# Layer 1's projection of two tiles by seven block products in place of eight

## Chip, core and metric

The kernel runs on one core of one Trainium2 chip. The metric is the device time of one execution in microseconds (us). The engines are named as in the profile: PE (matrix products; PEld is its weight load), DVE (vector), ACT (scalar and tables), POOL (which here issues the gathers) and SP (which issues the other transfers).

## The reference

Two graph attention layers follow one another on 3327 nodes with 1024 features. Each layer's output is added to its input, and the sum is normalized over the features.

```
# layer 0: 8 heads of 128
h = x @ W0;  e[h,i,j] = leaky(h_i . a_src[h] + h_j . a_dst[h]);  masked by adj
x = layernorm(x + softmax(e) @ h)
# layer 1: one head
h = x @ W1;  e[i,j] = leaky(h_i . a1 + h_j . a2);  masked by adj
x = layernorm(x + relu(softmax(e) @ h))
```

The adjacency matrix is sparse (about 0.5% set, plus the diagonal). All data are fp32.

## The kernel before, in words

The 3327 rows are cut into 26 tiles of 128 (`NT`). The program has three stages. The first projects x with W0 (L475), turns the adjacency into lists of edges and stores the projected rows in `h0_d`. A flag then picks one of two forms; with this input it is `sparse` (L743), which does layers 0 and 1 with gathers.

In `sparse` each target tile has four blocks of 4 x 128 edges (`NG` = 4 groups of 32 targets) and a last block of 128 edges. `gather` (L800) fetches the source row of every edge by indirect DMAs, 17 per tile, on POOL's queue. Blocks share five buffers `src0` to `src4`. `weights` makes the attention weights of one block on DVE, and `sums` multiplies them with the gathered rows on PE.

Layer 1 (`Target`, L940) first aggregates the normalized rows y, and then projects: (attention @ y) @ W1 is the same as attention @ (y @ W1). `sums` (L987) adds up three cuts of 342, 342 and 341 columns in three banks. `close` (L998) divides by the sum of the weights and adds the node's own row; the result is z. `finish` (L1015) transposes z in two halves on PE (L176, copied to `xT` by ACT, L179), multiplies xT by W1, which stands in SBUF as `wt1` (eight blocks of 128 rows), in two halves of 512 columns (L1025), and applies maximum and residual on DVE (L1028). `settle` (L1033) normalizes and stores.

`prepare` (L946) loads a tile's own rows y, makes the marks that say which edge belongs to which target (L819, L823), and brings the target's scores into the layout of `way`, by a transposition (L949) and an exponential (L951). `way` is one bank of PSUM which holds small intermediate values for both layers.

The order of all work is written out by hand in `pipeline` (L1038), under a manual schedule: every engine executes its instructions in the order in which they are emitted, and waits for the data of the others. For tile t and block b, it emits in this order: at block 0 the `close` of tile t-1, then `late` steps of the queue `work`; `prepare` of tile t+1 at block 2; `own` at block 0; `weights` of block b+1; `sums` of block b; the gathers of block b of tile t+1; `behind[b]` steps of `work`; and one step of `ahead`. `work` holds the generators `finish`, `ahead` the generators `settle` (and, at first, `score_weights`, L767). A step runs to the next `yield`. In layer 1 a tile's `finish` has ten steps, two for the transpositions and eight for a quarter of a half projection each; `late` is 1 and `behind` is (2, 2, 2, 2, 1).

PSUM has eight banks. Before, tag A has five of them (accumulators of both layers), S one (projection, and layer 0's denominator), T one (transpositions), and E one (`way`). In layer 0 the two accumulators of a tile come from A, in layer 1 the three.

Of the kernel before, what the change touches and what calls it, by code (L numbers as in the profile page):

```python
# [19 lines left out]
P = 128  # L20
# [6 lines left out]
def kernel(  # L27
# [43 lines left out]
    EB = 4  # L71
# [671 lines left out]
    def sparse(own):  # L743
        ph = Phase(own, "sparse", {"A": 5, "S": 1, "T": 1, "E": 1})
# [20 lines left out]
        wa = [pool.tile([P, D], F32, bufs=1, name=f"wa{n}") for n in range(2)]  # L765

        def score_weights():  # L767
            for n, a in enumerate((a1_src, a1_dst)):
                av = sbuf("z", [P, D], 3, "av")
                spread(av, a)  # L770
                for k in range(KT):
                    pr = sbuf("pr", [P, D], 1)
                    nc.vector.scalar_tensor_tensor(
                        pr, wt1[:, k, :], 1.0, av, op0=OP.mult, op1=OP.mult, accum_out=wc[:, n, k : k + 1]
                    )
                    if k % 3 == 2:
                        yield
# [48 lines left out]
        class Layer0:  # L826
# [5 lines left out]
            def prepare(self):  # L832
# [4 lines left out]
                self.h = sbuf("own", [P, HW0], 2)  # L837
# [14 lines left out]
            def begin(self):  # L852
                self.acc = [bank("A", [P, 4, DH], "acc") for _ in range(2)]
# [4 lines left out]
            def weights(self, b):  # L858
# [10 lines left out]
                e = sbuf("e", [P, H * P], 3).rearrange("p (g h t) -> p g h t", g=ng, h=H)  # L869
# [45 lines left out]
            def finish(self):  # L915
# [13 lines left out]
                for n in range(2):  # L929
                    pr = sbuf("pr", [P, D], 1)  # L930
                    nc.vector.scalar_tensor_tensor(  # L931
                        pr, y, 1.0, wa[n], op0=OP.mult, op1=OP.mult, accum_out=r1.sd[:, t, n, :]
# [7 lines left out]
        class Target:  # L940
# [5 lines left out]
            def prepare(self):  # L946
                t = self.t
                tr = bank("T", [P, P], "tr")
# [6 lines left out]
                self.res = ys[t % 3]  # L955
# [15 lines left out]
            def begin(self):  # L971
                self.acc = [bank("A", [P, CUTS[1]], "acc1") for _ in range(3)]
# [25 lines left out]
            def close(self):  # L998
# [5 lines left out]
                z = self.z = sbuf("z", [P, D], 3)  # L1004
# [10 lines left out]
            def finish(self):  # L1015

                t, z, res = self.t, self.z, self.res
                xT = sbuf("xT", [P, KT, P], 2)
                yield from ph.transposed(xT, z, (0, 1))
                o = sbuf("z", [P, D], 3, "o")  # L1020
                for g in range(2):
                    half = slice(g * HALF, (g + 1) * HALF)
                    acc = bank("S", [P, HALF], "mm")
                    for k in range(KT):
                        nc.tensor.matmul(acc, xT[:, k, :], wt1[:, k, half], start=k == 0, stop=k == KT - 1)  # L1025
                        if k in (1, 3, 5):
                            yield
                    nc.vector.scalar_tensor_tensor(o[:, half], acc, 0.0, res[:, half], op0=OP.max, op1=OP.add)  # L1028
# [203 lines left out]
```

## Time and profile before

| | us |
|---|---|
| median of 3 runs | 1957.28 (1956.42 to 1968.05) |
| profiled execution | 1903.19 |
| its span, first to last instruction | 1901.5 |
| PE busy | 1518.5 (80%) |
| DVE busy | 1146.6 (60%) |
| POOL busy | 1030.2 (54%) |
| ACT busy | 546.6 (29%) |
| PE, projection of layer 1 (L1025) | 383.3, 832 records |
| PE, sums of layer 1 (L993) | 206.2, 2496 records |

The profile is of one execution, taken by the hardware profiler. Times in it count from the span's start. Layer 0's gathers begin at 482 us, those of layer 1 at 1198.6; layer 1 ends with the span. An fp32 product of one weight block appears as two matmul records. Busy time of PE is modelled, since its products are pipelined; the chain of waits shows their real spacing. The chain follows the work that ended last back to what released it.

### The profile page before, as it was taken

The numbers are of one execution on the slowest core, as the hardware profiler recorded it, in microseconds if no ns is written. First come the engines' busy times: TensorE is split into PE (matmuls) and PEld (weight loads), VectorE is DVE, ScalarE is ACT, GpSimd is POOL, SyncE is SP. The second block draws the span as 40 slices with busy tenths as digits, with TensorE's granted clock in tenths as the row PEclk, the third lists the DMA queues.
The fourth block names the chain that finished last, engine by engine and source line by source line (L and its number), as shares of the span: only waits on it lengthen the run. The fifth ranks groups of instructions, "written<-read, shape, count | busy, mean of one in ns | idle before, by whom it ended". The sixth has DMA issues, their size and how long they took to land.

```text
span 1901.5 us, 38079 instructions
## 1 busy us (share of the span) xinstructions
PE 1518.5 (80%) x14663; PEld 902.4 (47%) x14663; DVE 1146.6 (60%) x3058; ACT 546.6 (29%) x1422; POOL 1030.2 (54%) x1391
## 2 busy tenths in 40 slices
PE   8799999999266555656556565399999999999997
PEld 5465556666255554545545454144444444444443
DVE  6699999986386665666666666244444444444442
ACT  5544455542022222222222222012222212222220
POOL 4322222220576666676676764677766667666650
PEclk9899999999678777787788877699999999999999
DMA  7656455411899999999999997899999999999980
GB/s 184 101 133 131 100 99 99 88 62 39 325 373 404 396 392 394 366 405 392 386 392 389 394 376 273 332 398 410 400 372 382 380 378 369 359 371 373 366 326 33
DMA packets 171068, 567.76 MB, mean 299 GB/s; under 512 B 27690, under 2 KB 34346, under 8 KB 170878
## 3 DMA queue, kind: packets, MB, share of 16 engines
q0 software_dynamic: 131056, 455.68, 67.6%
q1 hardware_dynamic: 39822, 109.56, 15.4%
q8 instruction: 118, 1.93, 0.4%
q14 instruction: 72, 0.59, 0.1%
HBM read 578.85 MB, written 42.97 MB: 327 GB/s over the span
## 4 chain that ended last, share of the span: by engine, by line
PE 52%; DMA 24%; DVE 12%; ACT 6%; issue 4%; POOL 2%; SPq 0%; DVEq 0%; ACTq 0%; POOLq 0%
DMA src<-h_d,idx 20%; PE mm L1025 20%; PE acc L993 12%; PE mm L479 12%; DVE e L870 3%; PE acc L898 3%; ACT junk L311 3%; PE tr L176 2%; POOL src L803 2%; DMA src<-y_d,idx 2%; DVE pr L931 1%; PE acc L882 1%; DMA wt<-in_L_gnn_W_dram 1%; ACT xT L179 1%; PE xp L411 1%
## 5 line engine op out<-in xcount | busy, mean ns | idle before, releaser
L803 POOL DMA_INDIRECT src<-h_d,idx x416 | 441.1, 1060 | 209.1 <-PE acc L898 58.0
L803 POOL DMA_INDIRECT src<-y_d,idx x416 | 415.7, 999 | 221.6 <-PE acc L993 96.3
L898 PE MATMUL acc<-src,e 128*32 128x128 f32 x6656 | 278.5, 337 | 253.6 <-DVE e L870 253.5
L479 PE MATMUL mm<-wt,xT 128*128 128x347 f32 (+1 forms) x1248 | 402.3, 469 | 3.3 <-DMA wt<-in_L_gnn_W_dram 2.9
L1025 PE MATMUL mm<-wt,xT 128*128 128x512 f32 x832 | 383.3, 604 | 0.8 <-DVE o L1028 0.8
L898 PEld LDWEIGHTS acc<-src,e 128*32 128x32 f32 x6656 | 234.8, 137 | 311.3 <-DVE e L870 284.3
L479 PEld LDWEIGHTS mm<-wt,xT 128*128 128x128 f32 x1248 | 228.3, 192 | 106.0 <-issue 4.2
L1025 PEld LDWEIGHTS mm<-wt,xT 128*128 128x128 f32 x832 | 152.2, 190 | 199.5 <-issue 179.1
L993 PE MATMUL acc<-src,es 128*32 128x342 f32 (+1 forms) x2496 | 206.2, 464 | 33.8 <-DVE es L984 31.0
L870 DVE TENSOR_TENSOR e<-oh,way 128x1024 f32<-128x1024 f32 x130 | 158.7, 1221 | 63.2 <-ACT w L868 62.8
L993 PEld LDWEIGHTS acc<-src,es 128*32 128x32 f32 x2496 | 71.6, 111 | 158.6 <-issue 112.9
L868 ACT ACTIVATE w<-way 128x32 f32<-128x32 f32 (+1 forms) x130 | 24.6, 189 | 407.7 <-DVE way L866 395.6
L1028 DVE SCALAR_TENSOR_TENSOR o<-mm,y 128x512 f32<-128x512 f32 x52 | 35.9, 691 | 166.2 <-PE mm L1025 166.2
L1007 ACT ACTIVATE z<-y,ri 128x342 f32<-128x342 f32 (+1 forms) x78 | 39.5, 570 | 313.9 <-DVE ri L1003 313.9
L865 DVE TENSOR_TENSOR way<-src,re 128x32 f32<-128x32 f32 x104 | 20.8, 200 | 175.1 <-DMA src<-h_d,idx 157.6
L179 ACT ACTIVATE xT<-tr 128x512 f32<-128x512 f32 x104 | 59.4, 596 | 151.0 <-PE tr L176 150.9
L981 DVE TENSOR_TENSOR way<-way,src 128x128 f32<-128x128 f32 x104 | 31.1, 299 | 90.0 <-ACT way L951 44.2
L850 ACT ACTIVATE own<-own,es 128x128 f32<-128x128 f32 x208 | 63.6, 388 | 57.4 <-DVE es L847 57.4
L311 ACT ACTIVATE junk<-ad 128x3328 uint8<-128x3328 uint8 x26 | 78.4, 3014 | 2.5 <-POOL ad L308 2.5
L882 PE MATMUL acc<-end,e 128*128 128x128 f32 x416 | 67.7, 328 | 13.3 <-DVE e L870 13.3
L296 POOL CAST mvs<-r 128x8 bf16<-128x8 f32 x26 | 6.0, 232 | 122.8 <-ACT r L295 122.8
L335 POOL TENSOR_TENSOR place_of<-cnt 128x1 f32<-128x1 f32 x26 | 4.9, 190 | 121.0 <-ACT cnt L328 101.5
(188 smaller groups left out, 1959.7 us busy)
## 6 DMA issues: line engine op xcount, KB each, us to landing
h_d<-ht SPq DMA_DIRECT2D x26, 520.0 KB
own<-h_d SPq DMA_DIRECT2D x26, 520.0 KB
y_d<-y SPq DMA_DIRECT2D x26, 514.0 KB
y<-y_d SPq DMA_DIRECT2D x26, 514.0 KB
x<-in_x_dram SPq DMA_DIRECT2D x25, 512.0 KB
y<-in_x_dram SPq DMA_DIRECT2D x25, 512.0 KB
out_dram<-o SPq DMA_DIRECT2D x25, 512.0 KB
ad<-in_adj_dram POOLq DMA_DIRECT2D x25, 415.9 KB
```

The costliest lines, as they stand in the source:

```text
L176: nc.tensor.transpose(tr[:, k, :], src[:, (4 * g + k) * P : (4 * g + k + 1) * P], ident)
L179: nc.scalar.activation(part, tr, AF.Copy)
L311: nc.scalar.activation(junk, ad, AF.Copy, accum_out=self.deg)
L479: nc.tensor.matmul(acc, xT[t][:, k, :], wt[:, k, CUTS0[c] : CUTS0[c + 1]], start=k == 0, stop=k == KT - 1)
L803: nc.gpsimd.indirect_dma_start(out=s[:, g, :w], out_offset=None, in_=table[:, :], in_offset=bass.IndirectOffsetOnAxis(ap=idx[:, t, b * NG ...
L850: nc.scalar.activation(hn, hn, AF.Copy, scale=es[:, n : n + 1])
L870: nc.vector.tensor_tensor(e, oh.unsqueeze(2).to_broadcast([P, ng, H, wide]), wp.unsqueeze(3).to_broadcast([P, ng, H, wide]), OP.mult,)
L882: nc.tensor.matmul(self.acc[h // 4][:, h % 4, :], e[:, 0, h, :], rowsof[:, 0, h, :], start=False, stop=h % 4 == 3,)
L898: nc.tensor.matmul(self.acc[h // 4][g * GT : (g + 1) * GT, h % 4, :], e[:, g, h, :], rowsof[:, g, h, :], start=first and h % 4 == 0, stop= ...
L993: nc.tensor.matmul(self.acc[c][to, :m], es[:, g, :], s[:, g, CUTS[c] : CUTS[c + 1]], start=b == 0, stop=b == EB,)
L1007: nc.scalar.activation(z[:, cut], self.res[:, cut], AF.Copy, scale=ri[:, 1:2])
L1025: nc.tensor.matmul(acc, xT[:, k, :], wt1[:, k, half], start=k == 0, stop=k == KT - 1)
```

## The change

Two consecutive tiles of layer 1, an even one a and an odd one b, are projected together. With xT and W1 each cut into blocks of half the inner dimension and half the columns, four blocks of the result take eight products of blocks in the plain way. The new code makes seven, after Strassen in Winograd's form. Each has four inner blocks of 128, so 16 steps of `finish` with two inner blocks each become 14.

- `combine_weights` forms four combinations of the blocks of W1, once, between the two layers. They are kept in `on_marks` with `prod` (t2, t3), in `owns` (t4), and in `wt1` itself (w12). These are buffers which layer 0 has used.
- `first` makes two products for the even tile: the first one is copied to u2 by ACT, the second gives a's first half.
- `second` makes four combinations of xT on DVE, five products, and from these b's two halves and a's second half. A half is finished by `put`: one addition, and the maximum with the residual, in place in the tile's rows `res`.
- `settle` normalizes in place in `res`. The rows y of layer 1 have five buffers in place of three (the two vectors `wa` of layer 0 get reused), z has one in place of three, and the vector `av` of `score_weights` has one as well.
- The banks: A 3, S 3, T 1, E 1. Layer 1's accumulators use the three of A, its products those of S. In layer 0 the accumulators take A and A, or A and S, in turn. The transposition of the scores in layer 1's `prepare` writes to a free quarter of `way`.
- `pipeline` takes other numbers of steps for even and odd tiles, the first being `late`: (2, 1, 1, 2, 2, 2) and (2, 2, 1, 2, 1, 0). `lag=4` puts four empty steps first; no steps are taken behind tile 0. Layer 0 keeps its steps.

```diff
-        ph = Phase(own, "sparse", {"A": 5, "S": 1, "T": 1, "E": 1})
+        ph = Phase(own, "sparse", {"A": 3, "S": 3, "T": 1, "E": 1})
...
-        wa = [pool.tile([P, D], F32, bufs=1, name=f"wa{n}") for n in range(2)]
+        was = [pool.tile([P, HW], F32, bufs=1, name=f"wa{n}") for n in range(2)]
+        wa = [w[:, :D] for w in was]
+        owns = [pool.tile([P, HW0], F32, bufs=1, name=f"own{n}") for n in range(2)]
+        on_marks = [pool.tile([P, D], F32, bufs=1, name=f"e{n}") for n in range(3)]
+        prod = pool.tile([P, D], F32, bufs=1, name="prod")
+        HK = KT // 2
+        w11, w12 = wt1[:, :HK, :HALF], wt1[:, :HK, HALF:]
+        w21, w22 = wt1[:, HK:, :HALF], wt1[:, HK:, HALF:]
...
+        def combine_weights():
+            for n in range(2):
+                k = slice(2 * n, 2 * n + 2)
+                nc.vector.tensor_tensor(t3[n], w22[:, k, :], w12[:, k, :], OP.subtract)
+            nc.vector.tensor_tensor(w12, w12, w11, OP.subtract)
+            for n in range(2):
+                k = slice(2 * n, 2 * n + 2)
+                nc.vector.tensor_tensor(t2[n], w22[:, k, :], w12[:, k, :], OP.subtract)
+                nc.vector.tensor_tensor(t4[n], w21[:, k, :], t2[n], OP.subtract)
...
-                av = sbuf("z", [P, D], 3, "av")
+                av = sbuf("z", [P, D], 1, "av")
...
-                self.acc = [bank("A", [P, 4, DH], "acc") for _ in range(2)]
+                self.acc = [bank(tag, [P, 4, DH], "acc") for tag in ("AA", "AS")[self.t % 2]]
...
-                tr = bank("T", [P, P], "tr")
+                tr = way[:, 3 * P :]
...
-                self.res = ys[t % 3]
+                self.res = y1s[t % len(y1s)]
...
-                self.acc = [bank("A", [P, CUTS[1]], "acc1") for _ in range(3)]
+                self.acc = {c: bank("A", [P, CUTS[1]], "acc1") for c in (2, 0, 1)}
...
+                self.xT = sbuf("xT", [P, KT, P], 2)
+                turn = ph.transposed(self.xT, self.z, (0, 1))
+                next(turn)
+                yield
+                next(turn)
+                yield from self.second() if self.t % 2 else self.first()
+
+            def product(self, a, w):
+                self.p = bank("S", [P, HALF], "mm")
+                for k in range(HK):
+                    nc.tensor.matmul(self.p, a[:, k, :], w(k), start=k == 0, stop=k == HK - 1)
+                    if k == 1:
+                        yield
+
+            def put(self, g, u, p, room):
+                half = slice(g * HALF, (g + 1) * HALF)
+                nc.vector.tensor_tensor(room, u, p, OP.add)
+                nc.vector.scalar_tensor_tensor(
+                    self.res[:, half], room, 0.0, self.res[:, half], op0=OP.max, op1=OP.add
+                )
+
+            def first(self):
+                yield
+                yield from self.product(self.xT, lambda k: w11[:, k, :])
+                nc.scalar.activation(u2, self.p, AF.Copy)
+                yield
+                yield from self.product(self.xT[:, HK:, :], lambda k: w21[:, k, :])
+                self.put(0, u2, self.p, u4)
+                yield
+
+            def second(self):
+                before = tiles1[self.t - 1]
+                a, b = before.xT, self.xT
+                a1, a2, b1, b2 = a[:, :HK, :], a[:, HK:, :], b[:, :HK, :], b[:, HK:, :]
+                nc.vector.tensor_tensor(s1, b1, b2, OP.add)
+                nc.vector.tensor_tensor(s2, s1, a1, OP.subtract)
+                nc.vector.tensor_tensor(b1, a1, b1, OP.subtract)
+                nc.vector.tensor_tensor(a2, a2, s2, OP.subtract)
+                yield
+                yield from self.product(s2, lambda k: t2[k // 2][:, k % 2, :])
+                nc.vector.tensor_tensor(u2, u2, self.p, OP.add)
+                yield
+                yield from self.product(s1, lambda k: w12[:, k, :])
+                p5 = self.p
+                nc.vector.tensor_tensor(u4, u2, p5, OP.add)
+                yield
+                yield from self.product(b1, lambda k: t3[k // 2][:, k % 2, :])
+                nc.vector.tensor_tensor(u3, u2, self.p, OP.add)
+                self.put(1, u3, p5, u2)
+                yield
+                yield from self.product(b2, lambda k: t4[k // 2][:, k % 2, :])
+                self.put(0, u3, self.p, u3)
+                ahead.append(self.settle())
+                yield
+                yield from self.product(a2, lambda k: w22[:, k, :])
+                before.put(1, u4, self.p, u4)
+                ahead.append(before.settle())
+                yield
...
-                    run(work, behind[b])
+                    if t:
+                        run(work, behind[b])
...
-            pipeline(Layer0, 0, (1, 1, 1, 1, 1), get_edges)
-            pipeline(Target, 1, (2, 2, 2, 2, 1), lambda t: None)
+            pipeline([Layer0(t) for t in range(NT)], ((0, 1, 1, 1, 1, 1),) * 2, get_edges)
+            combine_weights()
+            tiles1 = [Target(t) for t in range(NT)]
+            y1s = ys + was
+            pipeline(tiles1, ((2, 1, 1, 2, 2, 2), (2, 2, 1, 2, 1, 0)), lambda t: None, lag=4)
```

## The prediction

> **What bounds the kernel now.** I read the windows by stage first, then the chain of waits inside layer 1, then the waits and the DMA rate. The windows (columns: window and its length, busy PE, PEld, DVE, ACT, POOL, granted clock, DMA share, GB/s):
>
> ```profile
> 480.00:840.00 360.00, 208.47 (x3985) 173.84 (x3989) 223.27 (x538) 81.62 (x242) 242.53 (x230) 0.77 1.00 384
> ...
> 1400.00:1540.00 140.00, 136.56 (x767) 58.80 (x766) 61.31 (x178) 30.80 (x54) 94.15 (x95) 1.00 0.99 378
> ...
> 1409.86:1435.41 25.55, 24.86 (x145) 10.68 (x144) 11.37 (x33) 5.84 (x12) 17.00 (x18) 1.00 0.99 371
> ```
>
> Layer 0 (480 to about 1193) has PE busy 58% and DMA full; the change's products are not there. Layer 1 has PE busy 97% at full clock, and DMA nearly full as well. The last row is exactly one layer-1 tile: 25.55 us, DVE busy 11.4. The chain through that tile (start, length, what):
>
> ```profile
> 1409.86 3.43 PE mm L1025 x8
> 1413.30 1.86 PE acc L993 x24
> 1415.16 0.60 PE tr L176 x4
> 1415.76 0.02 issue
> 1415.79 0.61 ACT xT L179
> 1416.39 0.04 issue
> 1416.44 0.66 PE tr L176 x4
> 1417.09 1.86 PE acc L993 x24
> 1418.95 3.63 PE mm L1025 x8
> ...
> 1433.68 1.73 PE acc L993 x6
> ```
>
> The reader is to see that one tile is PE work end to end, with one hole of 0.68 us (second transposition waiting for ACT). It gives the units: half a product P (four records) is 1.71 us; a pair of P is 3.43, or 3.63 directly after a sums block; sums S 1.86, last block E 1.73, transposition of half a tile T 0.66. From the waits and the rate at the start of layer 1, where POOL issues without pause:
>
> ```profile
> POOL src L803 <- PE acc L993: 91.4, 104, 3.7
> ACT xT L179 <- PE tr L176: 117.3, 42, 4.8
> PE tr L176 <- ACT xT L179: 14.5, 21, 0.7
> ...
> 1215.00:1220.00 5.00, 3.78 (x5) 0.63 1.03 416
> 1220.00:1225.00 5.00, 3.78 (x5) 1.00 1.03 410
> 1240.00:1245.00 5.00, 3.94 (x4) 1.00 1.02 408
> ```
>
> Gathers wait for PE to free their buffers, and no wait on a gather is left in steady layer 1. But the ceiling is near: about 410 GB/s. A tile moves 376 GB/s (mean of four tiles) x 25.55 us = 9.61 MB, so DMA alone needs 23.4 us per tile. POOL needs 17 gathers x 1.295 us between starts = 22.0.
>
> **What the Trainium skill says.** "Perfetto Trace Analysis", Identifying the Most-Contended Engine: PE's matmul busy share is a bad measure of headroom, since matmuls are pipelined. Hence I take spacing from the chain (0.43 us per record), not the 592 ns that one record shows; the trace agrees that these differ. "VectorE: DVE Perf Modes", Mode 2x_2P: an fp32 tensor_tensor stays at one element per cycle. The trace agrees: L870 takes 1.22 us for 1024, L819 0.68 for 512. "PSUM — Partial Sum Buffer", PSUM bank collisions raise a hardware error: two engines may not touch one bank at once, so accesses must be guarded by bank. The trace shows such a guard: DVE L981 waits for ACT L951, which writes other columns of `way` (40.6 us in 21 times).
>
> **The change, part by part.**
>
> *Products.* Per pair of tiles 14 P instead of 16. Before, a pair takes 51.1 us. After, in PE's order by the counts. Odd tile: P P (3.43), S, P P (3.63), S, T, S, T, P (1.75), S, P (1.91), E. Even tile: P P (3.43), S, T, S, T, S, P P (3.63), S, P P (3.63), E, P P (3.43). P sums to 24.8, eight S and two E to 18.3, four T to 2.65, the two score transpositions to 0.2: 46.0 us. The saving of 5.1 has two roots: 3.9 in products, 1.2 because the two T of a tile now have sums between them.
>
> *Additions on DVE.* Eleven tensor_tensor of 128x512 per pair more (four combinations of xT, three of u, four in put); the four maxima stay. Price 0.69 each (L1028 0.69, L819 0.68); 0.61 start to start if the next one does not depend on it, 0.72 if it does. Some 7.6 us per pair, so DVE goes from 11.4 to about 15.2 us per tile: not full, but in order. I walk it against PE:
> (a) Into the odd tile. After the third product of `second` DVE does u3 and put (0.1+0.72+0.72+0.61), and only then close (three small ones 0.6, ACT's first z, then three STT every 0.51). The first STT ends 3.9 us, the last 4.95 after that product; PE arrives at the sums after 3.43. Accumulators now have three banks, so all three wait: 0.57 us.
> (b) Odd tile, block 0 to 2. After the last product DVE does put (1.4), the statistics of one settle (1.7), then weights(2) (0.96) : 4.2 us. PE meanwhile has S and T, 2.5. The stall is 1.7; the score transposition, now in the bank of `way`, has to wait as well and adds 0.2 (bounds 0 and 0.3). 1.9 us.
> (c) Into the even tile: put, own, weights(1) 2.8 against S and T 2.5: 0.35.
> Other places hold, some barely: s2 is ready about when PE gets to it. Some 0.2 for that. Stalls 3.0 (bounds 1.5 and 4.5, if DVE's gaps are 20% smaller or such a place turns bad). Pair: 49.0, or 24.5 per tile, above DMA's 23.4. Gain 2.0 (51.1 - 46.0 - 3.0 = 2.1, rounded down for the tighter DMA); twelve pairs, 24.
>
> *ACT.* One copy u2 (0.6) per pair, beside PE's work; its covers are the P after it. If uncovered 0.6.
>
> *Start of layer 1.* combine_weights: 8192 elements per partition, six of 1.22 and one of about 2.4, 9.7 us on DVE. It is queued after the last normalization (1193.3), ahead of the marks. DVE waits 14.74 us there for the first gather (to 1208.9), marks take 1.0. It hides with 4 us to spare: 0 (bounds 0 and 9.7). Four empty steps keep tile 1 light; it then runs at the gathers' speed: 1.2 less.
>
> *End.* After the last sums PE had 3.43 + two T + 16 records x 2; now P P, two T, a wait for ACT, s1, s2 (2.2), and five products (17.1), then two settles one after the other (3.2 each) instead of one. I get 38.5 against 32.0 (1869.5 to 1901.5): +6.5.
>
> *Layer 0.* Own rows, marks and product buffers are the same rings under other names; accumulators return after two tiles instead of 2.5, den after two instead of one. No wait there names a free bank; 0. But av has one buffer: the load of the second vector waits for the last product of the first (530.2) and SP's later loads queue behind it; DVE then waits for it in front of tile 1's weights. Loads there take 4 to 12 us (y_d 4.1, own 11.9), before DVE needed it at 532.7. Later DVE is full until 560 and gathers pause. Bounds 0 and 6; I take 2.
>
> *Queues.* SP issues one load and one store per tile as before, two stores per pair close together. The load of y at block 2 has about 14.5 us until the next tile's own (18.5 before); nobody waited for it in 540 us, own<-h_d took 11.9 in layer 0. Nothing taken; a late one would stop DVE in front of weights(1).
>
> **Sum.** -24 - 1.2 + 6.5 + 2 = -16.7. Profiled: 1903.2 (span 1901.5 and 1.7 around it) to 1886.5. The median shown is 54 us above that execution, and no view says where these lie. Difference or ratio give 1940.6 and 1940.1: 1940.
>
> **Rivals.** A is the forecast: stalls 1.5 to 4.5 give 1921 to 1957.
> B, the stalls vanish, and the gathers become the bound: 23.4 per tile, pair 46.8, 12 x 4.3 = 51 less 7.3 of one-off costs: 1914. For it: DVE has 9 us per tile free even afterwards, so its backlog is short. Against: (a) and (b) come from the order of DVE's queue, which is fixed by the code, not from its load.
> C, slower: DVE's additions lie bare on PE's path at tile boundaries, since each accumulator has only one bank. All 7.6 bare: pair 53.7, +31 + 7.3 = +38: 1996. It decides from 4.5 us of stalls per pair (5.1 less 7.3/12). Against: places other than (a) to (c) have 3.4 us of products as cover.
> D, no gain: the 54 us of the timed runs are slow transfers. On layer 0's 700 us that is 7.7%, the ceiling becomes 381 GB/s, a tile 25.2 us: 24 x 0.35 = 8 less 7.3: 1957. For it: DMA at 0.99 already. Against: in the trace 410 holds in both layers.
> That seven products aren't made is ruled out: two in `first`, five in `second`, four blocks of 512 columns each.
>
> **Chances.** A 0.5, B 0.2, C 0.12, D 0.18. One per cent (19.6 us) is about what a measurement can tell from no change. Faster by more: B and two fifths of A, 0.40; same: the rest of A and D, 0.48; slower: C. Range 1914 to 1966: from B to a little over D; outside are C and a part of B.
>
> **What would show it.** Pair period near 49 instead of 51.1; waits of PE for DVE L982/L984 of about 1.9 at one block per pair and for DVE's z of 0.6; DVE about 63% in layer 1; gathers still waiting for PE; 38 us after the last sums; DVE's first weights of layer 1 not after 1209. Wrong if PE waits for gathers (B or D), or if stalls pass 4.5 per pair.

## The result, and the profile after

The changed kernel took 2026.64 us (median of six runs, 2018.09 to 2031.58); beside it the kernel before took 1960.4 (1952.59 to 1970.13). The ratio is 1.0338, interval 1.0315 to 1.0362: slower, against a forecast of 1940. The numbers below come from seven comparisons, each of which ran the kernel before beside a changed one: in two of them the kernel before took 1960 and 1984 us, in the other five 1900 to 1902, with no lower granted clock (in the second slower one 0.91 to 0.92, in the faster ones 0.90 to 0.92), and I call them the slower and the faster comparisons. The result above is a slower one. The profile of before (1903) is of the faster kind, its median (1957) of the slower.

The windows of the changed kernel's first profile (2028.36 us, span 2026.6, from the slower comparison), in the stages shown of before (window and length; busy PE, PEld, DVE, ACT, POOL, each with its number of instructions; granted clock, DMA share, GB/s):

```profile
480.00:840.00 360.00, 249.07 (x3633) 167.77 (x3634) 211.22 (x513) 76.62 (x227) 225.94 (x217) 0.82 0.97 363
1400.00:1540.00 140.00, 118.17 (x704) 49.46 (x707) 78.66 (x204) 27.12 (x54) 85.36 (x85) 1.00 0.89 332
```

Layer 1 has PE busy 84% and the transfers 89%: neither is full any more. Layer 0, which has no product of the change, has PE busy 69% where it was 58%, with fewer matmuls done. The waits in 1300 to 1820 (who waited for what: us in all, times, longest):

```profile
PEld acc L1028 <- issue: 115.2, 339, 7.1
POOL src L839 <- PE acc L1028: 103.5, 49, 11.2
...
ACT xT L179 <- PE acc L1028: 58.0, 15, 7.9
ACT xT L179 <- PE tr L176: 33.6, 9, 5.7
...
PE acc L1028 <- issue: 31.2, 15, 6.3
DVE u L1098 <- PE mm L1063: 25.1, 3, 12.7
ACT u L1078 <- PE mm L1063: 20.8, 3, 9.4
ACT u L1078 <- PE acc L1028: 19.2, 5, 5.5
```

The reader is to see two things. ACT's copy of a transposed half (L179) needs no matmul of the sums, and yet in 15 of its waits it was let go only when one of those, issued later, had ended; the same holds for five of the nine u2 copies (L1078). And PE stands for up to 6.3 us for "issue", for nothing that this view can name. By its records PE's work was done, but the others learned of it late. I call the time from the start of a product's last record to the start of what reads it the hand-over. The chain that ended last, where it passes through two tiles (start, length, what):

```profile
1504.03 6.91 PE mm L1063 x16
1510.94 2.46 issue
1513.40 1.93 PE acc L1028 x24
1515.33 3.64 PE mm L1063 x8
...
1519.00 0.69 DVE u L1070
...
1519.72 0.69 DVE y L1071
1520.41 1.21 DVE st L192 x2
...
1522.73 0.29 DVE es L1019
...
1523.16 0.29 PE way L984
...
1532.49 11.04 DMA src<-y_d,idx
1543.53 0.29 DVE way L1016
```

Before, a tile was PE work end to end. Here PE has a hole of 2.5 us for "issue" ahead of a tile's first sums; then it waits through DVE's addition, maximum, statistics and weights, which is step (b) of the prediction; and then a gather that was issued late lands 11 us after its issue.

The hole has a cause, which the timeline shows (start, length, instruction, idle time before it and its releaser; "remote" is one that the view can't name):

```profile
1505.58 1.88 PE L1063 MATMUL mm<-prod,xT 128*128 128x512 f32 x4
...
1509.48 0.69 DVE L1101 TENSOR_TENSOR u<-u,mm 128x512 f32<-128x512 f32 x1 [4.15 <-remote]
...
1512.72 1.54 DVE L1045 SCALAR_TENSOR_TENSOR z<-acc,ri,z 128x340 f32<-128x340 f32 x3 [0.65 <-ACT z L1042]
...
1513.40 1.93 PE L1028 MATMUL acc<-src,es 128*32 128x341 f32 x24 [2.51 <-issue]
```

The first line is the second half of the product that u3 (L1101) reads. Its last record started at 1506.87, and u3 began 2.6 us later, though DVE had idled for 4.15 us. Behind u3 in DVE's queue stand a `put` and the `close` (L1045), which has to read the accumulators before PE may write the next tile's sums into them. This holds for every pair: PE's gap at this place is u3's hand-over less 0.11 us in each of the 12 pairs of this profile that have a next tile, from 0.52 to 6.35 us and 3.3 on average. It is step (a) of the prediction, priced there at 0.57.

The same changed kernel was profiled again in a faster comparison (1894.6 span), and there the stages and the waits read:

```profile
480.00:840.00 360.00, 207.42 (x3970) 169.91 (x3970) 221.57 (x537) 81.47 (x241) 239.08 (x228) 0.77 0.99 382
1400.00:1540.00 140.00, 131.35 (x770) 56.60 (x769) 81.55 (x213) 26.20 (x54) 98.05 (x95) 0.99 1.00 388
```

```profile
ACT xT L179 <- PE tr L176: 78.8, 23, 4.8
PEld acc L1028 <- issue: 71.2, 353, 0.8
POOL src L839 <- PE acc L1028: 57.4, 80, 3.1
...
ACT u L1078 <- PE mm L1063: 50.9, 11, 5.1
...
PE way L984 <- DVE sg L197: 17.6, 10, 1.8
```

Every copy is now released by the matmul that it needs, and no gather waits over 3.1 us for its buffer. The hand-over to ACT's u2 copy took 0.63 us in 12 of 13 cases (0.69 in the other) here; in the first profile 0.63 to 6.64, 2.54 on average. The hand-over to u3 took 0.63 in all 13 cases here, there 0.63 to 6.47, 3.22 on average; and PE's gap ahead of the next tile's sums is 0.52 to 0.59 here in every pair.

### The profile page after: what moved, and what is told of

Its sections match the earlier page's. It is cut to its first block, busy times and chain, and to the rows that moved or that the text cites. A ratio compares the mean times of both kernels' runs of the same rounds, so it can differ in the third digit from the quotient of the medians.

```text
span 2026.6 us, 37944 instructions
## 1 busy us (share of the span) xinstructions
PE 1633.9 (81%) x14559; PEld 917.0 (45%) x14559; DVE 1241.4 (61%) x3208; ACT 520.8 (26%) x1411; POOL 1034.7 (51%) x1391
## 4 chain that ended last, share of the span: by engine, by line
PE 62%; issue 15%; DVE 11%; DMA 5%; ACT 5%; POOL 2%; another core or an unknown queue 0%; SPq 0%; DVEq 0%; POOLq 0%; ACTq 0%
PE acc L934 16%; PE mm L1063 15%; PE mm L479 11%; PE acc L1028 9%; PE acc L918 4%; DMA src<-y_d,idx 3%; PE acc L926 3%; ACT junk L311 2%; POOL src L839 2%; PE tr L176 2%; DVE st L192 1%; DMA wt<-in_L_gnn_W_dram 1%; PE den L943 1%; PE xp L411 1%; DVE top L274 1%
## 5 line engine op out<-in xcount | busy, mean ns | idle before, releaser
L839 POOL DMA_INDIRECT src<-y_d,idx x416 | 425.1, 1022 | 300.7 <-PE acc L1028 139.3
L934 PE MATMUL acc<-src,e 128*32 128x128 f32 x6656 | 376.2, 297 | 177.6 <-issue 150.6
L1028 PE MATMUL acc<-src,es 128*32 128x342 f32 (+1 forms) x2496 | 231.1, 488 | 104.1 <-issue 47.6
L479 PEld LDWEIGHTS mm<-wt,xT 128*128 128x128 f32 x1248 | 228.2, 192 | 107.9 <-DMA wt<-in_L_gnn_W_dram 5.9
L1063 PE MATMUL mm<-wt,xT 128*128 128x512 f32 x312 | 149.0, 614 | 0.7 <-issue 0.7
L179 ACT ACTIVATE xT<-tr 128x512 f32<-128x512 f32 x104 | 59.3, 593 | 150.6 <-PE acc L1028 79.5
L918 PE MATMUL acc<-end,e 128*128 128x128 f32 x416 | 92.7, 411 | 2.6 <-DVE e L906 1.8
L1063 PEld LDWEIGHTS mm<-wt,xT 128*128 128x128 f32 x312 | 57.9, 196 | 72.5 <-issue 70.2
L918 PEld LDWEIGHTS acc<-end,e 128*128 128x128 f32 x416 | 85.8, 314 | 3.9 <-DVE e L906 1.9
L1070 DVE TENSOR_TENSOR u<-u,mm 128x512 f32<-128x512 f32 x52 | 35.6, 684 | 58.6 <-PE mm L1063 52.2
L926 PE MATMUL acc<-own,ident 128*128 128x512 f32 x104 | 66.3, 723 | 2.2 <-ACT own L886 2.2
L1042 ACT ACTIVATE z<-y,ri 128x342 f32<-128x342 f32 (+1 forms) x48 | 24.3, 570 | 164.2 <-DVE ri L1038 156.5
```

Source lines behind the costliest of these rows:

```text
L179: nc.scalar.activation(part, tr, AF.Copy)
L479: nc.tensor.matmul(acc, xT[t][:, k, :], wt[:, k, CUTS0[c] : CUTS0[c + 1]], start=k == 0, stop=k == KT - 1)
L839: nc.gpsimd.indirect_dma_start(out=s[:, g, :w], out_offset=None, in_=table[:, :], in_offset=bass.IndirectOffsetOnAxis(ap=idx[:, t, b * NG ...
L918: nc.tensor.matmul(self.acc[h // 4][:, h % 4, :], e[:, 0, h, :], rowsof[:, 0, h, :], start=False, stop=h % 4 == 3,)
L926: nc.tensor.matmul(self.acc[b - 1].rearrange("p h d -> p (h d)"), ident, self.h[:, (b - 1) * HALF : b * HALF], start=False, stop=False,)
L934: nc.tensor.matmul(self.acc[h // 4][g * GT : (g + 1) * GT, h % 4, :], e[:, g, h, :], rowsof[:, g, h, :], start=first and h % 4 == 0, stop= ...
```

## The experiments

"Pair" below is the time from one tile's `close` to that of the second next, on DVE, averaged over nine pairs in the middle of layer 1. "End" is from the start of the last sums' last record to the end. A ratio is that of a run's median to the median of the kernel before in the same comparison, with its 95% interval. e7, e8, e11, e12 and e14 leave out or replace a part of the data, so that they compute other numbers; only their times are read.

**The kernel before and the changed one, unchanged (e1, e10, e6).**

> The kernel before, unchanged, for a second profile of it. Its first profile (1903) lies 50 us below its median of 1957 to 1960. If layer 0 is what differs, its stretch (711 us in the first profile of before, about 748 us in the profile of after) should come out near 748 here and the whole near 1957; then layer 0 of after lost nothing by the change and all of the loss is in layer 1. If layer 0 comes out at 711 again, the change made layer 0 some 37 us slower.

> The kernel before, unchanged, for a profile of it on a chip of the slower kind. On such a chip (before 1960 to 1984, changed 2027) PE's counter moves in steps of 0.71 us while gathers run. If layer 0 is as long there for both kernels (about 735 us against 684 on the faster kind) and layer 1 takes 26.5 us per tile against 25.3, then the whole loss of the changed kernel (28.4 us per tile) is in layer 1. On a chip of the faster kind it repeats 1902.

> The changed kernel, unchanged, for a second profile and a second comparison with the kernel before on one chip. The kernel before took 1960 beside the changed kernel's 2027, but 1902 beside the first four experiments, and those four lie at 1899 to 1916; so the loss may belong to the changed kernel or to the place of that first comparison. Theory A (the three-fold wait holds PE's completions back): slower than before by 3% again wherever it runs: about 1965 beside 1902. Rival (the loss came with the slower conditions of the first comparison, under which layer 0's matmuls already came out in groups of four): beside a kernel before of 1902, the changed kernel takes 1895 to 1915 and its wait for three semaphores costs nothing that shows.

Measured: before 1901.1 and 1899.3, both in faster comparisons, pair 51.1, end 30.7, layer 0 from first to last sums 677 to 685 us. The changed kernel took 1897.3 beside 1900.8, ratio 0.9978 (0.9965 to 0.9992): pair 50.1, end 38.2, layer 0 684. In its first profile it had pair 57.1, end 38.2 and layer 0 722. So in a faster comparison the change is worth a fifth of a per cent, and layer 0 is untouched by it. The loss of 3.4% belongs to the slower comparisons; e3 and e9 below, which differ little from the changed kernel, lose 3.2 and 3.3% in the second of these. No run profiled the kernel before in a slower comparison with all its gathers.

**Is it the banks?** One bank for each accumulator lets all sums of a tile wait for the division of the tile before (my rival C), and gives PE a wait for three semaphores at once, in which its sequencer stood for 136 us in all between 1300 and 1850.

Banks alone (e2), in the kernel before:

```diff
-        ph = Phase(own, "sparse", {"A": 5, "S": 1, "T": 1, "E": 1})
+        ph = Phase(own, "sparse", {"A": 3, "S": 3, "T": 1, "E": 1})
...
-                self.acc = [bank("A", [P, 4, DH], "acc") for _ in range(2)]
+                self.acc = [bank(tag, [P, 4, DH], "acc") for tag in ("AA", "AS")[self.t % 2]]
```

> The kernel before, with its eight plain products and its old order, but with the accumulators laid out as in the changed kernel: three banks for layer 1's three sums, three for the products. If the banks are the loss, through the wait of a tile's first sums for the division of the tile before (by either mechanism, bare division or held-back completions), it loses 2 to 4 us per tile: 2010 to 2060. If the loss comes from Strassen's additions on DVE, it stays at 1957 to 1970.

Measured, in a faster comparison: 1902.6 beside 1902.0, ratio 1.0007 (0.9997 to 1.0017).

Five accumulator banks and one for the products (e4), four and two (e3), in the changed kernel; named banks taken in turn (`acc1` and `mm1` hand them out):

```diff
-                self.acc = {c: bank("A", [P, CUTS[1]], "acc1") for c in (2, 0, 1)}
+                self.acc = {c: acc1([P, CUTS[1]], "acc1") for c in (2, 0, 1)}
...
-                self.p = bank("S", [P, HALF], "mm")
+                self.p = mm1([P, HALF], "mm")
...
-                self.put(1, u3, p5, u2)
+                self.put(1, u4, self.p, u2)
```

> The changed kernel with the old banks: five in turn for the accumulators of both layers, one for the products, and the one addition that needed two products at once written over u4 instead. Theory (accumulator banks): two of three sums find a free bank at a tile's start, the three-fold wait is gone, layer 1 falls from 30 to 25 us per tile: 1900 to 1950, unless the single product bank costs 1 to 2 us per tile in place of it: 1950 to 1970. Rival (Strassen's additions on DVE hold PE wherever the banks lie): 2000 to 2030.

> The changed kernel with four banks in turn for layer 1's accumulators and two for the products, layer 0 with its old banks. The first sums of a tile then need the division of the tile before for two of three accumulators only, and no wait for PE's own count. Where the kernel before takes about 1901, theory (gathers bind layer 1, banks don't matter): 1893 to 1900. Rival (the boundary stalls bind): 1880 to 1890. Where the kernel before takes about 1960 as in the first comparison: 1950 to 1975 if the single accumulator banks made the loss there, 2015 to 2035 if not.

Measured: e4, in a faster comparison, 1915.8 beside 1902.0, ratio 1.0082 (1.006 to 1.0104). The waits that it was to remove cost nothing there, and the single product bank costs more (PE's matmuls, 1300 to 1820; busy and mean ns, then idle time before them and its releaser):

```profile
L1073 PE MATMUL mm<-own,xT 128*128 128x512 f32 x80 | 36.7, 601 | 15.9 <-DVE u L1080 15.9
```

e3 met a slower comparison: 2046.9 beside 1984.4, ratio 1.0324 (1.0269 to 1.0378), pair 56.3. With four banks the loss is that of the changed kernel. At place (a) PE stood for 1.0 us per pair, in place of 3.4 in the changed kernel's first profile, but it stood for another 1.0 ahead of a product whose bank u4 had yet to free, and longer ahead of other sums. So the banks decide where a late hand-over is felt, and their number alone is not the cause. Five banks met no slower comparison.

Accumulators kept, so that PE no longer waits for its own count, that is, for the semaphore that its own finished matmuls raise (e5):

```diff
-                self.acc = {c: bank("A", [P, CUTS[1]], "acc1") for c in (2, 0, 1)}
+                if not kept:
+                    kept.update({c: bank("A", [P, CUTS[1]], "acc1") for c in (2, 0, 1)})
+                self.acc = kept
```

> The changed kernel with its banks and order, but layer 1's three accumulators are one tile kept for all targets in place of one newly taken for each, so that a tile's first sums wait for a gather and DVE alone and no longer for PE's own count as well; what DVE and PE compute and in which order is the same. Theory A (PE stands in the wait for three semaphores ahead of time and its completions reach DVE and ACT late): most of the loss goes, 1930 to 1970. Theory B (the division lies bare because each sum has one bank): nothing changes, 2015 to 2035.

Measured, in a faster comparison: 1898.6 beside 1902.0, ratio 0.9984 (0.9977 to 0.9991). By itself this looks like the recovery of theory A; but e6, the same without the edit, gave 0.9978, with the same 136 us of standing in that wait. The wait costs nothing in a faster comparison. In a slower one it was not taken out alone; e3, whose profile doesn't have it either, lost as much.

**Does the traffic matter?** One gather in four of layer 1 left out, in both kernels, and, by itself, a plain last pair in the changed kernel (e7, e8; e9; the same slower comparison as e3):

```diff
-            for g in range(NG if b < EB else 1):
+            for g in range((NG if table is h0_d else NG - 1) if b < EB else 1):
```

```diff
-                yield from self.second() if self.t % 2 else self.first()
+                yield from self.alone() if self.t >= NT - 2 else self.second() if self.t % 2 else self.first()
```

> The kernel before, with one of the four gathers of each block of layer 1 left out (its quarter of the rows keeps what layer 0 left there, so layer 1's sums are other numbers): a quarter less is fetched, and all arithmetic stays. PE is busy 97.5% of layer 1 here, so little can be won: 1885 to 1900, if PE is the bound; under 1880 only if the gathers bind and PE's records overstate it.

> The changed kernel with the same gathers left out. Theory (layer 1 of the changed kernel now waits for its gathers, the DMA engines being 99% busy): with a quarter less to fetch the saved products show, 23.5 to 24.0 us per tile in place of 24.8, so 1865 to 1880, and the lead over the kernel before with the same gathers grows from 4 us to 15 or 25. Rival (the stalls at the tile boundaries eat the gain: score transposition behind DVE, first sums behind the division): 1890 to 1898, the lead stays at about 4.

> The changed kernel, but the last pair of tiles is projected each by itself with four plain products (w12 now holds the difference of two blocks, so the first product is added back in), so that after the last sums only one tile's products are left. The stretch after the last sums should fall from about 38 us to 31 or 33, at the cost of one more product (1.7 us) ahead of it: 4 to 6 us faster than the changed kernel's 1897, 1891 to 1894. If the end is set by normalising and storing two tiles and not by PE: no change.

Measured: e7 1961.8 and e8 1966.4, beside 1984.4 (ratios 0.9889, 0.9852 to 0.9925, and 0.9922, 0.9896 to 0.9949); e9 2050.3, ratio 1.0334 (1.0294 to 1.0375). The windows of layer 1, e7, then e8:

```profile
1300.00:1820.00 520.00, 506.25 (x2912) 217.01 (x2905) 226.53 (x663) 117.02 (x201) 265.97 (x265) 1.00 0.80 288
```

```profile
1300.00:1820.00 520.00, 471.67 (x2743) 201.67 (x2738) 287.76 (x752) 92.46 (x187) 266.77 (x260) 0.97 0.81 283
```

With 283 GB/s in place of 332 the changed kernel's pair falls from 57.4 (e9) to 52.8, and its distance from the kernel before from 66 us (first comparison) to 5. The hand-over to u3 is back at 0.63 in every pair (3.1 on average in e9), and with it PE's gap at place (a) at 0.52; the u2 copy still came after 1.71 us on average, and PE stood for 2.05 us per pair ahead of the first product of `second`. So the late hand-overs go with the gathers' traffic. The kernel before's pair is 51.1, to the hundredth what it is in a faster comparison; its 52 hand-overs of a product to DVE took 0.64 us on average, as in a faster one (0.63). Why it stays clear of them at a rate at which the changed kernel does not is not shown.

Layer 0 took 734 and 737 us in the two kernels, so it is slow there in both alike. All its gathers are made in e7 too, so that e1 and e7 show the same work in a faster and a slower comparison:

```profile
840.00:1180.00 340.00, 202.75 (x4043) 168.62 (x4043) 214.69 (x519) 84.19 (x247) 226.34 (x216) 0.80 1.00 383
```

```profile
840.00:1180.00 340.00, 249.75 (x3727) 169.96 (x3721) 198.38 (x485) 79.45 (x234) 216.26 (x207) 0.85 0.98 362
```

The DMA engines are as good as full in both, and in the slower one they move less. There the transfers themselves are slower, whatever the change does. In e9 the end stayed at 38 us: it seems that the last but one tile's products were not through in time.

As many gathers, of rows three quarters as long (e14, changed kernel):

```diff
+        short_y = y_d[:, :].rearrange("a b -> (a b)")[: NP * (HW * 3 // 4)].rearrange("(a b) -> a b", b=HW * 3 // 4)
...
-                self.src[b] = gather(y_d, HW, self.t, b)
+                self.src[b] = gather(short_y, HW * 3 // 4, self.t, b)
```

> The changed kernel with as many gathers in layer 1 as before, each of rows three quarters as long (read from a denser view of the table, so layer 1's sums are other numbers). With a gather in four left out the changed kernel lost nearly all of its disadvantage on the slower chip (1966 beside 1984). Theory (bytes): the same here, 1960 to 1975 beside 1984, and 1870 to 1885 beside 1902. Rival (the number of gathers, with their descriptors and completions): no gain on the slower chip, 2030 to 2050.

Measured, in a faster comparison: 1869.8 beside 1899.6, ratio 0.9836 (0.9802 to 0.987). The gain isn't in the steady loop (pair 49.6 for 50.1): the first `close` comes at 1210.0 in place of 1233.4, since the first tile is fetched sooner. In a faster comparison the gathers don't bind the loop. Whether the bytes or the number of gathers makes the trouble in a slower one stays open; this run met none.

**What do the additions cost?** Seven products without additions, in the kernel before (e11); the changed kernel without its seven additions s1, s2, b1, a2, u2, u4, u3 (e12):

```diff
-                    for k in range(KT):
-                        nc.tensor.matmul(acc, xT[:, k, :], wt1[:, k, half], start=k == 0, stop=k == KT - 1)
+                    last = KT // 2 - 1 if g and self.t % 2 else KT - 1
+                    for k in range(KT):
+                        if k <= last:
+                            nc.tensor.matmul(acc, xT[:, k, :], wt1[:, k, half], start=k == 0, stop=k == last)
```

```diff
-                nc.vector.tensor_tensor(s1, b1, b2, OP.add)
-                nc.vector.tensor_tensor(s2, s1, a1, OP.subtract)
-                nc.vector.tensor_tensor(b1, a1, b1, OP.subtract)
-                nc.vector.tensor_tensor(a2, a2, s2, OP.subtract)
...
-                yield from self.product(s2, lambda k: t2[k // 2][:, k % 2, :])
-                nc.vector.tensor_tensor(u2, u2, self.p, OP.add)
+                yield from self.product(a1, lambda k: t2[k // 2][:, k % 2, :])
...
```

> The kernel before, with the last four of the 32 matmuls of each pair of tiles left out (half of the sum over k of one half of the odd tile is missing from the result), so PE does seven products per pair without a single addition more on DVE. Theory (on the slower chip the additions' hand-overs between PE and DVE make the loss): it is faster than the kernel before on either chip, by 8 to 14 us. Rival (the saved PE time itself is worthless or harmful, since the gathers then run ahead and collide): no faster than the kernel before on the slower chip.

> The changed kernel without Strassen's additions (the four ahead of the products and three of those behind them; the products take blocks of the projected tile directly, so the result is another one); banks, order, product count and the waits of the products' readers stay. Theory (the additions' hand-overs make the loss): on the slower chip at or below the kernel before, 1940 to 1985 where that takes 1960 to 1984; on the faster 1885 to 1895. Rival (the order and the lag of the work make it): as slow as the changed kernel, 3% above the kernel before, on the slower chip.

Measured, in a faster comparison: e11 1855.7 beside 1899.6, ratio 0.9767 (0.9731 to 0.9803), pair 47.65; e12 1879.4, ratio 0.9885 (0.9851 to 0.9919), pair 49.1. Thirteen saved products of 3.43 us are 44.6, and e11 gets 43.8: all of it, far above my expected 8 to 14. PE stays full, and the transfers follow at 396 GB/s:

```profile
1300.00:1820.00 520.00, 504.89 (x3037) 216.42 (x3039) 247.49 (x720) 126.88 (x218) 363.21 (x364) 1.00 1.01 396
```

Of the 44 us the new order, its end and its waits, with the four additions that `put` keeps, take 24 (e11 to e12), the seven additions 18 (e12 to the changed kernel in e6, another faster comparison).

The additions in the kernel before, with all eight products: all eleven (e15), and only those ahead of the products (e18, the first part of the diff alone). `nil` holds zeros.

```diff
+                for k in (0, KT // 2):
+                    nc.vector.tensor_tensor(
+                        xT[:, k : k + KT // 2, :].rearrange("p k t -> p (k t)"),
+                        xT[:, k : k + KT // 2, :].rearrange("p k t -> p (k t)"), nil, OP.add,
+                    )
...
-                    nc.vector.scalar_tensor_tensor(o[:, half], acc, 0.0, res[:, half], op0=OP.max, op1=OP.add)
+                    nc.vector.tensor_tensor(u, acc, nil, OP.add)
+                    if g or t % 2:
+                        nc.vector.tensor_tensor(u, u, nil, OP.add)
+                    nc.vector.scalar_tensor_tensor(o[:, half], u, 0.0, res[:, half], op0=OP.max, op1=OP.add)
```

> The kernel before with its eight products per pair, banks and order, and with DVE additions of zero at the places and in the number of the changed kernel's: two on the transposed tile ahead of its products (four per pair), and behind each half tile's product one, for three of four halves two, before the last operation (seven per pair); the result is the same. Theory (the additions' hand-overs between PE and DVE make the loss): on a chip where the kernel before takes 1900 it loses 5 to 25 us, on a slower one (1960 to 1984) 3% or more, 2020 to 2060. Rival (order, lag and banks of the new arrangement make it): within 1% of the kernel before on either.

> The kernel before with the additions of zero ahead of the products alone (two on each transposed tile, four per pair), none behind them; the result is the same. PE stood 22.6 us in 520 for them with both kinds in, 1.1 us per tile. Theory (the additions ahead lie bare on PE's path): 30 to 38 us slower than the kernel before's 1900, nearly all of the 42. Rival (those behind the products make it, through DVE's queue): 5 to 15 us. On a slower chip (kernel before 1960 to 1984): 2 to 4% above the kernel before if late completions add to each hand-over, 1.5 to 2% if not.

Measured, in faster comparisons: e15 1941.8 beside 1899.9, ratio 1.021 (1.0187 to 1.0233), pair 53.5, end 36.5; e18 1906.3 beside 1899.7, ratio 1.0035 (1.0026 to 1.0044), pair 51.1. e15 loses 42 us, more than the 5 to 25 expected of it. PE's waits in e15:

```profile
PEld mm L1033 <- DVE xT L1024: 35.1, 20, 1.9
PE mm L1033 <- DVE xT L1024: 22.6, 20, 1.3
```

L1024 is the addition ahead of the products. Alone it costs the loop nothing; with additions behind the earlier product queued ahead of it on DVE, PE waits for it once per tile. DVE is busy only 56% of that window. It is the order in its queue that costs here, not a full engine. The additions behind the products were not run alone.

**Taking the order's stall away (e16, e19), and with e9's plain last pair (e17).** In layer 1 the normalizing step comes ahead of the products' steps in a block, so that a tile's statistics no longer stand in DVE's queue between a `put` and the next weights:

```diff
+                    if lag and (t or b):
+                        run(ahead)
                     if t:
                         run(work, behind[b])
-                    if t or b:
+                    if not lag and (t or b):
                         run(ahead)
```

> The changed kernel, with one swap in layer 1: in each block the step of normalising (statistics, scale, store) is issued ahead of the products' steps and no longer behind them, so that a tile's statistics, 1.4 us on DVE, start a block later and no longer stand between the addition behind a product and the next weights. Of the 2.0 us for which PE stands before block 2 of each odd tile it takes 1.4 to 1.7: 13 pairs, so 15 to 22 us, 1876 to 1883 where the changed kernel takes 1897. If the wait only moves to the next block: 1893 to 1900. On a slower chip (changed kernel 2027 to 2050) 1990 to 2040.

> The same swap, and the last pair of tiles by four plain products each, with more steps in the last tile's blocks so that the last but one tile is through when the last sums end: the stretch after the last sums falls from 38 us to 31 or 32, half of it paid ahead of them. 3 to 6 us below the swap alone: 1870 to 1880 where the changed kernel takes 1897.

> The changed kernel with the step of normalising issued ahead of the products' steps in each block, once more. On a chip where the kernel before takes 1900: 1881 again. On a slower one (kernel before 1960 to 1984): 1990 to 2035, faster than the changed kernel by about as much (16 us) and still slower than the kernel before; at or below the kernel before if the stall that the swap takes away is what the slower chip stretches.

Measured, in faster comparisons: e16 1881.0 beside 1899.9, ratio 0.9898 (0.9882 to 0.9915), pair 48.6; e19 1880.6, ratio 0.9897 (0.9865 to 0.9929). PE's 17.6 us of waiting at L984, shown above, have become:

```profile
PE tr L176 <- ACT xT L179: 10.2, 10, 1.0
...
PE way L984 <- DVE es L1019: 1.9, 1, 1.9
```

This version beats both kernels where the kernel before takes 1900; it met no slower comparison. e17 gives 1884.5 (0.9918, 0.9902 to 0.9935), no gain over the swap alone: the end is 6 us shorter, but the last pair, with more products in it, takes 59.7 us where it took 48.3.

## Why the prediction was wrong

**Products**: nearly right. PE's own work in a pair was to be 46.0 us; in the faster comparison it is 93.3% of 50.1, 46.8. The saving is real (e11).

**Additions on DVE**: stalls of 3.0 us per pair, bounds 1.5 and 4.5. This is the step that failed. In the faster comparison it was near: PE idles 34.8 us in 520, 3.4 per pair, and (b) was the largest and in the right place, 1.9 foreseen at block 2 of the odd tile, 17.6 us in 10 pairs measured; the swap wins back 1.5 per pair. In the slower comparison, in which the result was measured, PE idles 79.4 us in 520, 8.7 per pair, nearly three times the forecast, and its own work is drawn out to 48.4. The groups of PE with the difference (busy and mean ns, then idle before them and its releasers), first profile, then second:

```profile
L1028 PE MATMUL acc<-src,es 128*32 128x342 f32 (+1 forms) x1752 | 154.0, 479 | 45.5 <-issue 27.9 <-DVE es L1019 8.9 <-PE mm L1063 3.4
L1063 PE MATMUL mm<-e,s 128*128 128x512 f32 x72 | 33.3, 605 | 13.8 <-issue 6.7 <-DVE s L1089 5.9 <-DVE s L1088 1.2
```

```profile
L1028 PE MATMUL acc<-src,es 128*32 128x342 f32 (+1 forms) x2016 | 166.7, 464 | 15.1 <-DVE es L1019 9.9 <-PE mm L1063 5.3
L1063 PE MATMUL mm<-e,s 128*128 128x512 f32 x82 | 38.1, 606 | 2.1 <-DVE s L1089 1.9 <-issue 0.2
```

(b) is unchanged, 1.76 us in each pair in both. Over nine pairs in the middle of layer 1, what grew is (a), from 0.5 to 3.4 us per pair, and the place of which I wrote "s2 is ready about when PE gets to it" (the second line of each fence), from 0.2 to 1.4. I had priced each hand-over from PE to DVE at 0.1 us after the product's end, the value of the one profiled execution, and walked DVE against PE with covers of some tenths of a microsecond. In the slower comparison those behind four of the seven products (u2, the addition to u2, u4, u3) were 1.5 to 3.8 us longer on average, and for u3 the excess comes out on PE in full. My own mark, from 4.5 us of stalls per pair it is slower, was passed.

**Start, end, layer 0**: the end is 7.5 us longer than the 30.7 of e1 and e10, 5.9 longer than that of the profile of before, against 6.5 foreseen; layer 0 and `combine_weights` show nothing beyond the 7 us by which two profiles of the kernel before differ.

**Sum**: in the faster comparison the loop gave twelve times 0.95 us in place of 24, since the pair fell to 50.1 and not to 49.0; of these 1.1 us, 0.8 are PE's own work and 0.3 stalls. Less the longer end that is 4 us of gain, as measured beside 1901. The carrying over failed as well: I moved the whole difference from an execution of 1903 to a median of 1957, as though the 54 us between them lay where the change doesn't reach.

**Rivals**: C had the side and the consequence, additions bare on PE's path at the tile boundary where each accumulator has one bank. What it lacked is why: in the faster comparison they are largely covered, and in the slower one more banks only moved the stall (e3). D saw that the 54 us matter and took them for slow transfers. For layer 0 that fits: 362 GB/s for 383 with DMA engines as full, and 734 us for 685. In layer 1 the changed kernel's transfers are 89% busy, and PE's largest stall follows the hand-over to u3 and no gather; what slower transfers add beside it was not separated. B is out in the faster comparison: with a quarter of the bytes gone the pair is 0.5 us shorter, and e11 runs at 396 GB/s.

**What is shown, and what not**: shown are the late hand-overs in the slower comparisons, that they shrink with the gathers' traffic, that the one to u3 lies on the changed kernel's path, and that the kernel before, with fewer gathers, hardly has them. Shown too is that additions on DVE cost even without them, 18 us for seven of them in the changed kernel and 42 for eleven in the kernel before. That taking the additions out would mend the slower comparison is argued; e12, e15 and the swap met only faster ones. Open is what makes a comparison slower: the experiments ran on five chips, each comparison on one, and a single one of these was slow, so that nothing here tells the chip from the moment.

## What to carry over

A saved product pays only if what replaces it doesn't enter an in-order queue on which the product's neighbours wait: look at the order in that queue, not at its load alone, before counting PE's time. Slack of some tenths of a microsecond in a hand-over between engines may hold only in the execution that was profiled; where the median lies 3% above the profile, as here, part of the difference may be in just such hand-overs. When a view says "issue", follow the engine that the waiting one depends on back to its own late start. Put two profiles of the same program side by side before blaming an edit.

## What was not expected of the hardware

In the slower comparison PE's count, as the others see it, moved in steps. Of the gaps between successive changes of it, 246 lay within 0.66 to 0.76 or 1.35 to 1.50 us between 600 and 1100 us of the changed kernel's first profile, against 8 in its second; in layer 1 (1300 to 1800) 200 against 55. The kernel before has them in layer 0 too, 177 in e7 against 3 in e1. In stretches of layer 0 PE's matmuls came out in spells of four or five about every 0.73 us. Before 480 us, with transfers at some 100 GB/s, the steps are no more frequent than in the faster one. The Trainium skill, "TensorE: Matmul & The Clock Gate", The cost: per-tile semaphore tail, says that increments serialize, each being a write to one register, at 26.3 ns each. In both profiles the closest successive changes are 0.03 us apart, which fits; for the steps of the slower one the page has no price. "Perfetto Trace Analysis", Tensor Engine Instruction, says that a matmul's end in the profile is estimated, and that the count is pushed only when PSUM has acknowledged. This fits: the records of a product last some 0.6 us and start every 0.43 in both profiles, while the hand-over to the u2 copy went from 0.63 to as much as 6.64 us. Which part of the way from the matmul to the reader became slow, and why, is not shown.

The groups of layer 0's matmuls, first and second profile (count, busy and mean ns, idle before and its releaser):

```profile
L934 PE MATMUL acc<-src,e 128*32 128x128 f32 x6656 | 376.2, 297 | 177.6 <-issue 150.6
```

```profile
L934 PE MATMUL acc<-src,e 128*32 128x128 f32 x6656 | 279.3, 338 | 246.3 <-DVE e L906 246.1
```

The same matmuls wait for DVE in the second and for nothing that has a name in the first. And in the faster comparison a wait in which PE's sequencer stood for up to 8.1 us at a time, 136 us in all, cost nothing (e5): PE itself idled ahead of its sums for only 15.1 us of a window nearly as long, since matmuls issued before were still running.
